# A graph layer's recurrent gates on one Trainium2 core: one scheme of 26 products of 256 columns for gates r and z of a pair of batches

## The chip, the core and the metric

The kernel runs on one core of a Trainium2 chip. The core has a matrix engine (PE, with its weight loads listed apart as PEld), a vector engine (DVE), a scalar engine (ACT), a general engine (POOL) and an engine that issues transfers (SP); each works through its own queue in order, and semaphores tie the queues together. Matrix products land in PSUM, eight banks of 128 x 512 floats; everything else lives in SBUF. The metric is the device time of one execution, in microseconds (us). A smaller time is better.

## The reference

The input x holds 32 batches of 512 tokens by 256 channels, all in float32. After a layer norm and a ReLU (h), each batch goes through three branches that meet in a GRU cell:

```
xc     = transpose(h)
x_conv = relu(bn2(conv17(relu(bn1(conv1(xc))))) + xc)          # convolution branch
A      = exp(-dist(h @ w_se.T)) * adj
x_nmp  = A @ relu(h @ w_msg.T + b_msg)                         # message branch
gi     = concat(x_conv, x_nmp) @ w_ih.T + b_ih                 # 768 columns: r, z, n
gh     = h @ w_hh.T + b_hh
r      = sigmoid(gi_r + gh_r);  z = sigmoid(gi_z + gh_z)
n      = tanh(gi_n + r * gh_n)
out    = x + (1 - z) * n + z * h
```

## The kernel before

Work is staged. Up to 836 us the kernel prepares what the gates need, for two groups of 16 batches: norm, first convolution and a transform to frequencies (`first_part`), the products with the frequency weights and the message branch (`nodes`). In `first_part` of the second group it also combines the gate weights (`combine_weights`, L591): POOL sums and ACT copies on 384-column tiles, spread over 15 batches, and one store of 1344 KB to DRAM for each of the three inputs. What the last stage needs lies in DRAM: h (`HD`), x_nmp (`ND`), the convolution's spectrum (`YD`) and the combined weights (`WS`).

The last stage, from 836 us to the end, is a loop over 16 pairs of batches, and it is where the change is. For a pair p:

- `load_pair` brings h (tile `HP`, "hp" in the profile), x_nmp (`NP`, "np") and the spectrum (`YT`, "yt"). All are channel-major: four row blocks of 512 tokens, block 2*i+j for channel half i and batch j of the pair.
- `inverse` (L661) turns the spectrum back into x_conv: per batch and channel half five products into one bank, then one DVE operation (L673) and one ReLU on ACT (L675) into `CP` ("cp").
- `sums` (L655) makes four sums of blocks on POOL for each of the three operands (L659): with them a 2 x 2 by 2 x 2 block product takes seven products, not eight (Strassen's scheme in Winograd's form).
- `gates_rz` (L687) does gates r and z. For each gate o the seven products run over the three operands k (h, x_nmp, x_conv), each one matmul of 128 x 128 weights on 512 columns. Two gates with two batches each are the four schemes of seven: 2 x 7 x 3 = 42 matmuls. DVE adds (L700, L712, L720), ACT copies (L707) and sigmoids (L696) finish them.
- `gate_n` (L797) does gate n in the same way, 21 matmuls; h's part has a bank of its own since r multiplies it. For each of the four blocks (i, j) DVE does up to four operations (`scaled`, `closing`) and ACT a tanh (L820). Then come three DVE operations for each block, d = h - n (L851), d *= z (L871) and n += d (L872, `blend`).
- `finish` transposes the result back to tokens on DVE (L878), adds x (L883) and stores it.

The order of work is written out by hand (`manual_schedule`): each engine runs its instructions as the program emits them. In the loop (L1197) PE's order is gates r and z of p, then `inverse(p + 1)`, then gate n of p: x_conv of the next pair is done one gate ahead of its first use. Inputs `HP`, `NP` and `CP` have two buffers each, so POOL's twelve sums for p + 1 (eight at `between(1)`, four behind `inverse`) never write where gates of p still read. `RZ` (r and z) has one buffer. A bank is taken by `bank(name)` from a pool of eight.

The last pair (p = 15) does r, then n, then z, with a tail of its own (`last_z`).

Of the kernel before, what the change touches and what calls it, by code (L numbers as in the profile page):

```python
# [15 lines left out]
P = 128  # L16
# [11 lines left out]
ROWS = 2 * UNITS  # L28

# [36 lines left out]
def gnn_layer(  # L66
# [168 lines left out]
    WS = [dram.tile([P, 7, 3, P], FP, name=f"ws_{k}") for k in range(K3)]  # L235
# [355 lines left out]
    def combine_weights():  # L591

        steps = []
        for k, src in enumerate((w_hhT, w_ihT[D:], w_ihT[:D])):
            w, t = (pools["sums"].tile([P, n, 3 * P], FP, tag=f"w{n}", name=f"w{n}_{k}", bufs=m) for n, m in ((4, 1), (7, 2)))
# [14 lines left out]
            for (dst, x1, x2, op), kept in zip(  # L610
                ((Q5, a21, a22, ALU.add), (Q6, q[Q5], a11, ALU.subtract),
                 (Q7, a11, a21, ALU.subtract), (Q3, a12, q[Q6], ALU.subtract)),
                ((Q1, a11), (Q2, a12), (Q4, a22), None),
            ):
                steps.append([partial(nc.gpsimd.tensor_tensor, q[dst], x1, x2, op=op)])
                if kept:
                    steps[-1].append(partial(nc.scalar.copy, q[kept[0]], kept[1]))
            steps[-1].append(partial(nc.sync.dma_start, WS[k], t.rearrange("p q (g o) -> p q g o", o=P)))
        return steps

    def load_combined(sw, q0, q1):
        for k in range(K3):
            nc.gpsimd.dma_start(sw[:, k, q0:q1], WS[k][:, q0:q1])

    def load_pair(p, queue=nc.sync):
        YT[p] = [pools["ops"].tile([P, len(spans), D], FP, tag="yt", name=f"yt_{p}_{j}", bufs=4) for j in range(2)]
        HP[p] = pools["ops"].tile([P, 8, N], FP, tag="hp", name=f"hp_{p}")
        NP[p] = pools["ops"].tile([P, 7, N], FP, tag="np", name=f"np_{p}")
        for j in range(2):
            b = 2 * p + j  # L630
            queue.dma_start(HP[p][:, j:4:2], HD[b])
# [3 lines left out]
        for j in range(2):  # L635
            queue.dma_start(NP[p][:, j:4:2], ND[2 * p + j])

    def load_pair_x(p):

        XP[p] = []  # L640
        for b in (2 * p, 2 * p + 1):
            t = pools["work"].tile([P, N // 32, D // 4], FP, tag="x", name=f"xb_{b}", bufs=3)
# [7 lines left out]
    def operands(t, keep):  # L650

        t3 = 7 if keep else B12
        return [t[:, i, :] for i in (B11, 5, B21, t3, 4, 6, B22)]

    def sums(t, keep):  # L655
        t3 = 7 if keep else B12
        sub = ALU.subtract
        for dst, a, b in ((4, B12, B11), (5, B22, 4), (6, B21, 5), (t3, B22, B12)):
            nc.gpsimd.tensor_tensor(t[:, dst, :], t[:, a, :], t[:, b, :], op=sub)  # L659

    def inverse(p):  # L661

        CP[p] = pools["ops"].tile([P, 7, N], FP, tag="cp", name=f"cp_{p}")
        for j in range(2):
            for oc in range(DC):
# [7 lines left out]
                nc.vector.scalar_tensor_tensor(xc, bk, scale2[:, oc : oc + 1], HP[p][:, 2 * oc + j, :],  # L673
                                               op0=ALU.mult, op1=ALU.add)
                nc.scalar.activation(xc, xc, AF.Relu, bias=shift2[:, oc : oc + 1], scale=1.0)  # L675
        del YT[p]

    def into(bk, q, o, ks, terms, first, t=slice(0, N)):

        for i, k in enumerate(ks):  # L680
            nc.tensor.matmul(bk[:, t], sw[:, k, q, o, :], terms[k][q][:, t], start=(first and i == 0), stop=(i == len(ks) - 1),  # L681
                             skip_group_check=True)

    def temp(role, name):
        return pools["late"].tile([P, N], FP, tag=role, name=f"{role}_{name}", bufs=2)

    def gates_rz(p, terms, between, outs=range(2)):  # L687
        if 0 in outs:
            RZ[p] = pools["late"].tile([P, 2 * DC, 2, N], FP, tag="rz", name=f"rz_{p}", bufs=1)
# [43 lines left out]
    def last_z(p, terms):  # L733
# [13 lines left out]
        def turned(i, j, t=slice(0, N)):  # L747
            dst, (js, half) = d[:, i, j, t], places(i, t)
            nc.vector.tensor_mul(dst, dst, d[:, DC + i, j, t])
            if (p, j) not in OUT:  # L750
                OUT[p, j] = pools["late"].tile([P, N // 32, D // 4], FP, tag="o", name=f"o_{p}_{j}", bufs=2)
# [45 lines left out]
    def gate_n(p, terms, last):  # L797
        rz, o = RZ[p], 2
        NT[p] = nt = pools["late"].tile([P, DC, 2, N], FP, tag="nt", name=f"nt_{p}", bufs=2)
# [7 lines left out]
        def scaled(bk, other, other_i, i, j):  # L807

            n = nt[:, i, j, :]
            if other is None:  # L810
                nc.vector.scalar_tensor_tensor(n, bk, b_hn[:, i : i + 1], rz[:, i, j, :], op0=add, op1=mul)
            else:
                nc.vector.scalar_tensor_tensor(n, bk, b_hn[:, i : i + 1], other, op0=add, op1=add)
                nc.vector.tensor_mul(n, n, rz[:, i, j, :])
                nc.vector.tensor_add(n, n, other_i)

        def closing(bk, i, j):
            n = nt[:, i, j, :]
            nc.vector.tensor_add(n, n, bk)  # L819
            nc.scalar.activation(n, n, AF.Tanh, bias=b_in[:, i : i + 1], scale=1.0)  # L820
# [12 lines left out]
        scaled(x1[0], None, None, 0, 0)  # L833
        closing(x1[1], 0, 0)
        pair(Q7, x2, False)
        u3 = [temp("u3", f"n{p}_{k}") for k in range(2)]
        for k in range(2):
            nc.vector.tensor_add(u3[k], p1[k], x2[k])
        x3 = [bank(f"pn3_{p}_{k}") for k in range(2)]
        pair(Q5, x3, True)  # L840
        scaled(x3[0], u3[0], u3[1], 1, 1)
        closing(x3[1], 1, 1)
        pair(Q4, x2, False)
        scaled(x2[0], p1[0], p1[1], 1, 0)
        closing(x2[1], 1, 0)
        pair(Q3, x3, False)
        scaled(x3[0], u2[0], u2[1], 0, 1)
        closing(x3[1], 0, 1)
        for i, j in ((0, 0), (1, 1), (1, 0), (0, 1)):

            (nc.gpsimd if last else nc.vector).tensor_tensor(rz[:, i, j, :], HP[p][:, 2 * i + j, :], nt[:, i, j, :],  # L851
                                                             op=ALU.subtract)
            if last and j == 0:
                early_out(p, i, j)
            elif not last:

# [403 lines left out]
```

## Time and profile before

| | |
|---|---|
| median of 2 runs | 1801.93 us (1801.38 to 1802.48) |
| the profiled execution, whole | 1803.28 us |
| its span, first to last instruction | 1801.4 us, granted PE clock 0.999 |
| last stage, first matmul of `inverse(0)` to the end | 835.9 to 1801.4 us |
| gates r and z of one pair, first matmul to the next stage's first | 36.05 us (1140.12 to 1176.17) |
| `inverse` of one pair | 5.65 us (1116.45 to 1122.10) |
| gate n of one pair | 18.02 us (1122.10 to 1140.12) |
| store of combined weights, one operand | 1344 KB, 7.3 us to landing |
| load of h, x_nmp, spectrum (SP's queue) | 512 KB 6.1 us, 512 KB 8.8 us, 640 KB 6.7 us to landing, each twice a pair |

The table's times are of one execution. In the timeline a group of matmuls has the start of its first record and a length whose end is modelled and overlaps the next; the distance from one start to the next is what PE needs. A float32 matmul leaves two records. A line of the timeline is: start in us, length in us, engine, source line, operation, output and input tiles, shape, how many were merged, and in brackets the engine's idle time before it with what ended it.

### The profile page before, as it was taken

How to read it: one execution, taken by the hardware profiler on the slowest of the kernel's cores; microseconds unless marked ns; L12 is line 12 of the kernel's file. 1: busy time of each engine (PE TensorE's matmuls, PEld its weight loads, DVE VectorE, ACT ScalarE, POOL GpSimd, SP SyncE). 2: the span in 40 equal slices, each digit the busy share in tenths (PEclk: the TensorE clock that was granted, in tenths of full speed). 3: DMA queues.
4: the chain of work that ended last, by engine and by line, in shares of the span. 5: the costliest groups of instructions: out<-in, count | busy, mean ns of one | idle time of the engine just before them, and what ended most of it. 6: DMA issues, size and time to landing. Idle time of an engine off the chain costs nothing.

```text
span 1801.4 us, 21211 instructions
## 1 busy us (share of the span) xinstructions
PE 1786.5 (99%) x6974; PEld 1148.8 (64%) x6974; DVE 1209.5 (67%) x2242; ACT 635.8 (35%) x1348; POOL 789.7 (44%) x733
## 2 busy tenths in 40 slices
PE   8999999999999999999999999999999999999998
PEld 6677888888998888885554555455545554555443
DVE  7885877886996777873456645665566556655666
ACT  4556554553345544543221222122212221222121
POOL 3432877877334878786123133213321332133221
PEclk9999999999999999999999999999999999999999
DMA  9999989786769889879043234323442344224402
GB/s 257 307 296 232 243 237 231 227 220 203 243 224 224 245 217 234 245 201 319 5 123 106 47 93 123 111 49 86 123 116 55 74 123 116 65 65 123 122 21 51
DMA packets 307089, 288.27 MB, mean 160 GB/s; under 512 B 146764, under 2 KB 237420, under 8 KB 306596
## 3 DMA queue, kind: packets, MB, share of 16 engines
q1 hardware_dynamic: 296948, 261.44, 53.8%
q0 software_dynamic: 6592, 23.50, 4.2%
q10 hardware_dynamic: 3440, 1.97, 0.4%
q8 instruction: 56, 0.92, 0.2%
q14 instruction: 53, 0.43, 0.1%
HBM read 190.45 MB, written 96.40 MB: 159 GB/s over the span
## 4 chain that ended last, share of the span: by engine, by line
PE 94%; DVE 2%; issue 1%; DMA 1%; POOL 1%; ACT 1%; ACTq 0%; SPq 0%; DVEq 0%; POOLq 0%
PE pg L681 30%; PE pn L681 15%; PE py L400 12%; PE pn L555 10%; PE pm L451 6%; PE pc L336 6%; PE pc L669 5%; PE px L351 3%; PE pd L493 2%; PE pw L260 2%; PE phT L316 1%; PE pz L681 1%; PE pn L538 1%; PE psr L475 1%; DMA w2p<-in_w2T_dram 0%
## 5 line engine op out<-in xcount | busy, mean ns | idle before, releaser
L659 POOL TENSOR_TENSOR hp<-hp 128x512 f32<-128x512 f32 x64 | 80.5, 1269 | 414.6 <-DMA hp<-hd 324.4
L681 PE MATMUL pg<-hp,sw 128*128 128x512 f32 x434 | 221.8, 593 | 0.7 <-DVE rz L700 0.5
L681 PE MATMUL pg<-np,sw 128*128 128x512 f32 x434 | 221.6, 592 | 0.0
L681 PE MATMUL pg<-cp,sw 128*128 128x512 f32 x434 | 221.6, 592 | 0.0
L659 POOL TENSOR_TENSOR cp<-cp 128x512 f32<-128x512 f32 x64 | 80.6, 1269 | 227.4 <-ACT cp L675 226.2
L696 ACT ACTIVATE rz<-rz,brz 128x512 f32<-128x512 f32 x93 | 67.0, 721 | 260.2 <-DVE rz L700 260.2
L367 POOL TENSOR_TENSOR wsum<-wt 128x512 f32<-128x512 f32 x78 | 112.0, 1436 | 102.4 <-DMA wt<-wd 61.9
L400 PE MATMUL py<-wt,xf 128*128 128x256 f32 x640 | 154.2, 384 | 0.0
L681 PEld LDWEIGHTS pg<-hp,sw 128*128 128x128 f32 x434 | 82.2, 190 | 104.7 <-issue 97.8
L681 PEld LDWEIGHTS pg<-cp,sw 128*128 128x128 f32 x434 | 82.5, 190 | 103.8 <-issue 103.8
L681 PEld LDWEIGHTS pg<-np,sw 128*128 128x128 f32 x434 | 82.5, 190 | 103.8 <-issue 103.8
L400 PEld LDWEIGHTS py<-wt,xf 128*128 128x128 f32 x640 | 117.1, 190 | 34.9 <-issue 19.7
L503 DVE TENSOR_TENSOR A<-A,at 128x512 f32<-128x512 f32 x124 | 132.9, 1110 | 1.2 <-ACT A L499 1.1
L820 ACT ACTIVATE nt<-nt,vech 128x512 f32<-128x512 f32 x64 | 46.2, 722 | 236.1 <-DVE nt L819 236.1
L336 PE MATMUL pc<-w,hT 128*128 128x256 f32 x512 | 118.0, 383 | 0.9 <-DVE hT L320 0.9
L451 PE MATMUL pm<-wmsg,hq 128*128 128x259 f32 x512 | 117.5, 381 | 0.0
L681 PE MATMUL pn<-cp,sw 128*128 128x512 f32 x224 | 114.4, 592 | 0.0
L681 PE MATMUL pn<-np,sw 128*128 128x512 f32 x224 | 114.4, 592 | 0.0
L681 PE MATMUL pn<-hp,sw 128*128 128x512 f32 x224 | 114.4, 592 | 0.0
L336 PEld LDWEIGHTS pc<-w,hT 128*128 128x128 f32 x512 | 94.6, 190 | 24.2 <-issue 7.2
L451 PEld LDWEIGHTS pm<-wmsg,hq 128*128 128x128 f32 x512 | 96.5, 189 | 14.7
L669 PEld LDWEIGHTS pc<-back,yt 128*128 128x128 f32 x640 | 92.7, 190 | 7.7 <-issue 7.7
(175 smaller groups left out, 3373.5 us busy)
## 6 DMA issues: line engine op xcount, KB each, us to landing
wt<-wd SPq DMA_DIRECT2D x80, 512.0 KB, 7.4
adj<-in_adj_dram SPq DMA_DIRECT2D x128, 256.0 KB, 6.7
wd<-wst SPq DMA_DIRECT2D x64, 320.0 KB, 5.9
yd<-y SPq DMA_DIRECT2D x76, 256.0 KB, 5.1
yt<-yd SPq DMA_DIRECT2D x30, 640.0 KB, 6.7
hd<-hT SPq DMA_DIRECT2D x32, 512.0 KB, 4.5
nd<-nmp SPq DMA_DIRECT2D x32, 512.0 KB, 3.0
xb<-in_x_dram SPq DMA_DIRECT2D x128, 128.0 KB, 3.8
```

The source lines that it names most:

```text
L336: nc.tensor.matmul(p[:, j, :], HT[b][:, ic, c * P : (c + 1) * P], w1[:, ic, :], start=(ic == 0), stop=(ic == DC - 1))
L351: nc.tensor.matmul(p[:, j * 2 * L : (j + 1) * 2 * L], H1[b][:, c0 + j, ic * P : (ic + 1) * P], fwd, start=True, stop=True)
L367: nc.gpsimd.tensor_tensor(t, WT[g, u][:, 0], WT[g, u][:, 1], op=ALU.add)
L400: nc.tensor.matmul(dst, v[:, ic, :], w[:, ic, :], start=(ic == 0), stop=(ic == DC - 1))
L451: nc.tensor.matmul(p[:, : D + NS], hq[:, ic, c * P : (c + 1) * P], wmsg[:, ic, :], start=(ic == 0), stop=(ic == DC - 1))
L503: nc.vector.tensor_mul(A[b][:, mc, :], EXP.pop((b, mc)), AT.pop((b, mc)))
L555: nc.tensor.matmul(bk, left[:, k, :], right[:, k, :], start=(first and k == 0), stop=(k == 1), skip_group_check=True)
L659: nc.gpsimd.tensor_tensor(t[:, dst, :], t[:, a, :], t[:, b, :], op=sub)
L669: nc.tensor.matmul(bk[:, t0:t1], YT[p][j][:, c, oc * P : (oc + 1) * P], back[:, n : n + t1 - t0], start=(c == 0), stop=(c == len(spans) - ...
L681: nc.tensor.matmul(bk[:, t], sw[:, k, q, o, :], terms[k][q][:, t], start=(first and i == 0), stop=(i == len(ks) - 1), skip_group_check=True)
L696: nc.scalar.activation(rz[:, g, j, :], src, AF.Sigmoid, bias=brz[:, g : g + 1], scale=1.0)
L820: nc.scalar.activation(n, n, AF.Tanh, bias=b_in[:, i : i + 1], scale=1.0)
```

## The change

Gates r and z of a pair (p = 0 to 14) are computed as one block product, four output blocks (two gates, two halves) by two input halves by four column blocks of 256 tokens (two batches, two halves), in 26 products (`gates_rz26`). Each is three matmuls of 128 x 128 weights on 256 columns: 78 matmuls of 256 columns take the place of 42 of 512. `PRODUCTS` lists them in order: the operand, an earlier product onto whose bank it accumulates, ACT copies of a bank into a slot (t), DVE additions, and outputs that become a sigmoid one product later.

The operands are blocks of the inputs (b), halves of the four pair sums as before (t3, t4, r5, r6) and ten sums of blocks (E0 to E9). POOL makes all of them: for h and x_nmp together eight operations on 128 x 512 for the pair sums and ten on 128 x 2 x 256 for the E, and for x_conv four on 128 x 512 and ten on 128 x 256. `SUMS_AHEAD` is emitted ahead of gate n, `SUM_ORDER` behind `inverse(p + 1)`.

The tiles of sums (`TN`, `TE`, `TNC`, `TEC`), `CP`, `NT`, `RZ` and the output tile have one buffer each; h and x_nmp share a tile `HN` in two alternating places; `YT` and the x tile have two in place of four and three. `inverse(p + 1)` moves from in front of gate n to behind it, directly ahead of the next pair's gates. In gate n the DVE operations write intermediate values into banks, tanh goes into a bank, and the blends of blocks (0, 0) and (1, 1) are done between the products, those of (1, 0) and (0, 1) among the operations of `inverse(p + 1)`.

`combine_weights` makes 28 more weight blocks for each of the three operands (20 POOL sums and 8 ACT copies of 128 columns), in tiles of one buffer where the seven-product tile had two, and stores 448, 896 and 1664 KB an operand in place of 1344. The last pair keeps the seven-product schemes, its r and z weights loaded into the place of the 26 on SP's queue once gates r and z of pair 14 are done.

```diff
+PRODUCTS = (
+    ('b01', None, 't0=p0', '', ''),
+    ('b03', None, 't1=p1', '', ''),
+    ('b11', None, 't2=p2', 'c11=p2+t0', 'c11=c11'),
+    ('b13', 1, '', '', 'c33=p1'),
+    ('r5_1', None, '', 't3=t0-p4', ''),
+    ('E9', None, '', 't0=t1+p5', ''),
+    ('E8', None, 't1=p6', '', ''),
+    ('t3_1', None, '', 't4=p7-t1 t5=p7-t3', ''),
+    ('E4', None, '', 't1=p8-t0 c23=p8+t4', ''),
+    ('E6', None, '', 't6=p9+t2', ''),
+    ('E7', None, '', 't2=p10-t1', ''),
+    ('r6_0', None, '', 't1=p11-t2 c22=t1-t6', ''),
+    ('E5', None, 't7=p12', '', ''),
+    ('E3', 11, '', 'c21=p11-t6', ''),
+    ('t4_0', None, '', 'c12=p14-t6', ''),
+    ('r5_0', None, '', 't6=p15+t1', ''),
+    ('r6_1', None, '', 'c01=p16-t5', 'c01=c01'),
+    ('t4_1', None, '', 't1=t7+p17 c03=p17-t5', 'c03=c03'),
+    ('t3_0', None, '', 't5=p18-t6 c02=p18-t1', ''),
+    ('E2', None, '', 't6=p19+t4 t7=t6-t5 c12=c12+t7', 'c12=c12'),
+    ('E0', None, '', 'c10=p20-t7 c30=p20+t2', '-c10=c10 c30=c30'),
+    ('b00', None, '', 't2=p21-t6 c22=c22-t2 c23=c23-p21', 'c20=t2 -c23=c23'),
+    ('b13', 17, '', 'c13=p17+t3', 'c13=c13'),
+    ('b12', None, '', 't2=p23-t1 t3=t0-t2 c21=c21-t3', 'c21=c21 c31=t3'),
+    ('b10', 20, '', 'c00=p20+t5', '-c00=c00'),
+    ('E1', None, '', 't0=p25+t2 c02=c02+p25 c22=c22+t0', '-c02=c02 -c22=c22 c32=t0'),
+)
+BLOCK_SUMS = {
+    'E9': ('b11', '+', 'b12'),
+    'E0': ('b10', '-', 'E9'),
+    'E4': ('b00', '-', 'b03'),
+    'E8': ('E4', '+', 'b13'),
+    'E2': ('E8', '-', 'b10'),
+    'E7': ('E4', '-', 'E0'),
+    'E6': ('t4_0', '+', 'E0'),
+    'E5': ('b12', '-', 't4_1'),
+    'E1': ('b02', '-', 't4_1'),
+    'E3': ('E1', '-', 'E7'),
+}
+PAIR_SUMS = {"t4": (1, 0), "r5": (3, "t4"), "t3": (3, 1), "r6": (2, "r5")}
+SUMS_AHEAD = ("E9", "E0", "E4", "E8", "E2", "E7")
+SUM_ORDER = (
+    ('t3', 'hn'), ('t4', 'hn'), ('E6', 'hn'), ('E5', 'hn'), ('E1', 'hn'), ('E3', 'hn'), ('r5',
+    'hn'), ('r6', 'hn'), ('t4', 'c'), ('r5', 'c'), ('E9', 'c'), ('E4', 'c'), ('E8', 'c'), ('t3',
+    'c'), ('E0', 'c'), ('E6', 'c'), ('E7', 'c'), ('r6', 'c'), ('E5', 'c'), ('E1', 'c'), ('E3', 'c'),
+    ('E2', 'c'),
+)
...
-            w, t = (pools["sums"].tile([P, n, 3 * P], FP, tag=f"w{n}", name=f"w{n}_{k}", bufs=m) for n, m in ((4, 1), (7, 2)))
+            w, t, u = (pools["sums"].tile([P, n, m], FP, tag=f"w{n}", name=f"w{n}_{k}", bufs=1)
+                       for n, m in ((4, G // 2), (7, G // 2), (len(PRODUCTS) + 2, P)))
...
+            more = [partial(nc.gpsimd.tensor_tensor, block(dst), block(x), block(y), op=op)
+                    for dst, x, y, op in (v for text in WEIGHT_SUMS for v in terms_of(text))]
+            same = [partial(nc.scalar.mul, block(dst), block(x.lstrip("-")), -1.0 if x[0] == "-" else 1.0)
+                    for dst, x, y, op in (v for text in WEIGHT_COPIES for v in terms_of(text))]
...
+                steps[-1] += spread(more, n, 4) + spread(same, n, 4)
+            parts = t.rearrange("p q (g o) -> p q g o", o=P)
+            for dst, part in ((WN[:, :, k], parts[:, :, 2]), (WL[:, :, k], parts[:, :, :2]), (WH[:, :, k], u[:, : len(PRODUCTS)])):
+                steps[-1].append(partial(nc.sync.dma_start, dst, part))
...
+    def place_sums(p):
+        TN[p] = pools["tn"].tile([P, 4, 2, N], FP, tag="tn", name=f"tn_{p}", bufs=1)
+        TE[p] = pools["te"].tile([P, len(EXTRA), 2, HALF], FP, tag="te", name=f"te_{p}", bufs=1)
+        TNC[p] = pools["tnc"].tile([P, 4, N], FP, tag="tnc", name=f"tnc_{p}", bufs=1)
+        TEC[p] = pools["tec"].tile([P, len(EXTRA), HALF], FP, tag="tec", name=f"tec_{p}", bufs=1)
+
...
+    def sums_ahead(p):
+        for name in SUMS_AHEAD:
+            block_sum(p, name, "hn")
+
+    def sums(p, last):
+        for name, part in SUM_ORDER[p == 0 :]:
+            if not (last and name in BLOCK_SUMS):
+                block_sum(p, name, part)
+
...
+    def inverse(p, between=()):
+
+        between = list(between)
+        CP[p] = pools["cp"].tile([P, 4, N], FP, tag="cp", name=f"cp_{p}", bufs=1)
...
+                for step in between.pop(0) if between else ():
+                    step()
+        for step in (v for w in between for v in w):
+            step()
...
+    def gates_rz26(p, between):
+
+        rz = RZ[p] = pools["rz"].tile([P, 2 * DC, 2, N], FP, tag="rz", name=f"rz_{p}", bufs=1)
+        slots = CT.rearrange("p r (h n) -> p (r h) n", h=2)
+        banks, waiting = {}, []
+
...
+        for s, (name, onto, copies, adds, done) in enumerate(PRODUCTS):
+            if onto is None:
+                banks[s] = bank(f"pg_{p}_{s}")
+            bk = banks[s if onto is None else onto][:, :HALF]
+            hn, c = operand(p, name, "hn"), operand(p, name, "c")
+            for k in range(K3):
+                nc.tensor.matmul(bk, SW["hk"][:, s, k, :], c if k == 2 else hn[:, k], start=(onto is None and k == 0),
+                                 stop=(k == K3 - 1), skip_group_check=True)
+            for dst, src, *_ in terms_of(copies):
+                nc.scalar.copy(at(dst), at(src))
+            sigmoids()
+            for dst, x, y, op in terms_of(adds):
+                nc.vector.tensor_tensor(at(dst), at(x), at(y), op=op)
+            for word in done.split():
+                dst, src = word.lstrip("-").split("=")
+                waiting.append((dst, src, -1.0 if word[0] == "-" else 1.0))
+            for step in between.get(s, ()):
+                step()
+        sigmoids()
+
...
+        def finished(banks, other, spare, i, j):
+
+            n, r = nt[:, i, j, :], rz[:, i, j, :]
+            (bk, bk_i), (h, g) = banks, spare
             if other is None:
-                nc.vector.scalar_tensor_tensor(n, bk, b_hn[:, i : i + 1], rz[:, i, j, :], op0=add, op1=mul)
+                nc.vector.scalar_tensor_tensor(n, bk, b_hn[:, i : i + 1], r, op0=add, op1=mul)
+                nc.vector.tensor_add(n, n, bk_i)
             else:
-                nc.vector.scalar_tensor_tensor(n, bk, b_hn[:, i : i + 1], other, op0=add, op1=add)
-                nc.vector.tensor_mul(n, n, rz[:, i, j, :])
-                nc.vector.tensor_add(n, n, other_i)
+                nc.vector.scalar_tensor_tensor(h, bk, b_hn[:, i : i + 1], other[0], op0=add, op1=add)
+                nc.vector.tensor_mul(n, h, r)
+                nc.vector.tensor_add(g, other[1], bk_i)
+                nc.vector.tensor_add(n, n, g)
+            NEW[p, i, j] = n if last else g
+            nc.scalar.activation(NEW[p, i, j], n, AF.Tanh, bias=b_in[:, i : i + 1], scale=1.0)
 
...
-        scaled(x1[0], None, None, 0, 0)
-        closing(x1[1], 0, 0)
+        finished(x1, None, x1, 0, 0)
         pair(Q7, x2, False)
         u3 = [temp("u3", f"n{p}_{k}") for k in range(2)]
         for k in range(2):
             nc.vector.tensor_add(u3[k], p1[k], x2[k])
+        if not last:
+            for step in blend(p, 0, 0):
+                step()
         x3 = [bank(f"pn3_{p}_{k}") for k in range(2)]
         pair(Q5, x3, True)
-        scaled(x3[0], u3[0], u3[1], 1, 1)
-        closing(x3[1], 1, 1)
+        finished(x3, u3, x1, 1, 1)
         pair(Q4, x2, False)
-        scaled(x2[0], p1[0], p1[1], 1, 0)
-        closing(x2[1], 1, 0)
+        finished(x2, p1, x2, 1, 0)
+        if not last:
+            for step in blend(p, 1, 1):
+                step()
         pair(Q3, x3, False)
-        scaled(x3[0], u2[0], u2[1], 0, 1)
-        closing(x3[1], 0, 1)
...
+    def blend(p, i, j):
+        n, d = NEW.pop((p, i, j)), RZ[p][:, i, j, :]
+        return [partial(nc.vector.tensor_tensor, d, HN[p][:, 0, 2 * i + j, :], n, op=ALU.subtract),
+                partial(nc.vector.tensor_tensor, d, d, RZ[p][:, DC + i, j, :], op=ALU.mult),
+                partial(nc.vector.tensor_tensor, NT[p][:, i, j, :], d, n, op=ALU.add)]
 
...
+    homes = ("rz", "nt", "ct", "sw", "yt", "hn0", "te", "tn", "tnc", "tec", "cp", "hn1", "swn", "xb", "o")
+    with phase(*homes), tc.manual_schedule():
         pairs = B // 2
-        sw = pools["sw"].tile([P, K3, 7, 3, P], FP, name="sw")
+        CT = pools["ct"].tile([P, 6, N], FP, tag="ct", name="ct", bufs=1)
+        TURN, NEW = {}, {}
         load_pair(0, nc.gpsimd)
-        load_combined(sw, 0, 2)
-        sums(HP[0], True)
-        load_combined(sw, 2, 7)
-        sums(NP[0], False)
+        load_combined(0, 5)
+        place_sums(0)
+        sums_ahead(0)
+        load_combined(5, 12)
+        block_sum(0, *SUM_ORDER[0])
+        load_combined(12, 26)
+        load_n()
         inverse(0)
-        sums(CP[0], False)
+        sums(0, False)
         for p in range(pairs):
             more = p + 1 < pairs
-            if more:
-                load_pair(p + 1)
-            terms = [operands(HP[p], True), operands(NP[p], False), operands(CP[p], False)]
 
             def between(i):
                 if p > 0:
                     finish(p - 1, i)
                 if i == 1:
                     load_pair_x(p)
-                    if more:
-                        sums(HP[p + 1], True)
-                        sums(NP[p + 1], False)
-
+
+            terms = [operands(p, k) for k in range(K3)]
             if more:
-                gates_rz(p, terms, between)
-                inverse(p + 1)
-                sums(CP[p + 1], False)
+                steps = {4: [partial(load_pair, p + 1)]}
+                if p > 0:
+                    steps[3] = [partial(to_tokens, p - 1, 0, 0)]
+                    steps[5] = [partial(to_tokens, p - 1, 0, 1)]
+                    steps[6] = [partial(finish, p - 1, 0)]
+                    steps[7] = [partial(to_tokens, p - 1, 1, 0)]
+                    steps[8] = [partial(to_tokens, p - 1, 1, 1)]
+                    steps[9] = [partial(finish, p - 1, 1)]
+                steps[12] = [partial(load_pair_x, p)]
+                gates_rz26(p, steps)
+                place_sums(p + 1)
+                last = p + 2 == pairs
+                if last:
+                    load_last()
+                else:
+                    sums_ahead(p + 1)
                 gate_n(p, terms, False)
+                (s0, s1, s2), rest = blend(p, 1, 0), blend(p, 0, 1)
+                inverse(p + 1, [[s0], [s1], [s2], rest])
+                sums(p + 1, last)
```

## The prediction

> **What bounds the kernel now.** I read the page first: busy times and the chain that ended last.
>
> ```profile
> PE 1786.5 (99%) x6974; PEld 1148.8 (64%) x6974; DVE 1209.5 (67%) x2242; ACT 635.8 (35%) x1348; POOL 789.7 (44%) x733
> ...
> PE 94%; DVE 2%; issue 1%; DMA 1%; POOL 1%; ACT 1%; ACTq 0%; SPq 0%; DVEq 0%; POOLq 0%
> ```
>
> PE never stops, so the time is PE's own work, and a change has two terms: what PE has less to do, and where PE now has to wait. For the first, the timeline of PE, in the frequency products (256 columns) and in the gates (512):
>
> ```profile
> 421.80 1.89 PE L400 MATMUL py<-wt,xf 128*128 128x256 f32 x8
> 423.53 1.03 PE L400 MATMUL py<-wsum,both 128*128 128x256 f32 x4
> ...
> 1103.57 1.02 PE L681 MATMUL pg<-hp,sw 128*128 128x512 f32 x2
> 1104.43 1.02 PE L681 MATMUL pg<-np,sw 128*128 128x512 f32 x2
> ```
>
> From start to start, eight records (four matmuls) of 256 columns take 1.73 us, 0.4325 each; one of 512 takes 0.858. Half the columns cost half the time, with the same weight loads, so the shorter matmul has no penalty here.
>
> For the second term, the timeline of all engines where gate n of pair 14 ends. I call T the moment PE ends gate n, here 1737.34:
>
> ```profile
> 1730.67 0.75 DVE L813 SCALAR_TENSOR_TENSOR nt<-pn,vech,u_n 128x512 f32<-128x512 f32 x1 [0.17 <-PE pn L681]
> ...
> 1736.49 0.74 DVE L813 SCALAR_TENSOR_TENSOR nt<-pn,vech,u_n 128x512 f32<-128x512 f32 x1
> ...
> 1737.34 1.02 PE L681 MATMUL pg<-hp,sw 128*128 128x512 f32 x2
> ...
> 1738.79 0.69 DVE L819 TENSOR_TENSOR nt<-nt,pn 128x512 f32<-128x512 f32 x1
> 1739.39 0.68 DVE L851 TENSOR_TENSOR rz<-hp,nt 128x512 f32<-128x512 f32 x1
> ...
> 1741.45 0.69 DVE L851 TENSOR_TENSOR rz<-hp,nt 128x512 f32<-128x512 f32 x1
> ```
>
> From 1730.67 on DVE has no idle time: it ends gate n at T + 2.1 (1739.48), and then the blends, 2.06 us each (1739.39 to 1741.45), run beside the next pair's gates. Nobody waits for them. Later in the same timeline stand a wait for a one-buffer tile and a collision:
>
> ```profile
> 1748.57 2.13 POOL L872 TENSOR_TENSOR nt<-nt,rz 128x512 f32<-128x512 f32 x1
> 1750.74 0.69 ACT L696 ACTIVATE rz<-pg,brz 128x512 f32<-128x512 f32 x1 [9.98 <-POOL nt L872]
> ...
> 1769.51 0.69 DVE L815 TENSOR_TENSOR nt<-nt,u_n 128x512 f32<-128x512 f32 x1
> 1771.83 1.68 POOL L851 TENSOR_TENSOR rz<-hp,nt 128x512 f32<-128x512 f32 x1 [4.42 <-ACT nt L820]
> 1772.41 1.64 DVE L815 TENSOR_TENSOR nt<-nt,p_n 128x512 f32<-128x512 f32 x1
> ```
>
> The sigmoid writes block (0, 0) of the new `RZ`; POOL was reading other blocks of the old one. So a one-buffer tile comes free as a whole, after its last reader. And L815, two inputs in SBUF, takes 1.64 us beside a POOL sum, not 0.69, the sum 1.68, not 1.27.
>
> **PE's work.** 42 x 0.858 = 36.05 us become 78 x 0.4325 = 33.74: 2.31 us less a pair, 34.7 us over the fifteen pairs. That is 1.9% of 1801.9, and all that the change can give.
>
> **Where PE waits: x_conv comes late.** `inverse(p + 1)` now stands straight before the gates that read it, behind gate n on PE and DVE, and two blends move into gate n. DVE then ends gate n at T + 2.1 + 2 x 2.06 - 0.17 (its one gap) = T + 6.1. `inverse` takes PE 5.65 us; its first bank is full at T + 1.4, but the L673 that empties it queues behind gate n on DVE. L673 takes 0.75 and the ReLU 0.72, so the first x_conv block is there at T + 7.6. The first product wants it in its third matmul, at T + 5.65 + 2 x 0.4325 = T + 6.5: a wait of 1.2 with the hand-over. The second product wants the block that is emptied third; on DVE lie L673, blend step, L673, blend step, L673 (0.75, 0.72, 0.75, 0.73, 0.75), so T + 9.8, and 10.6 after the ReLU, where PE, late by 1.2, asks at T + 9.0: 1.6 more. So 2.8 us a pair is the least.
>
> Banks: a pair takes 22 in its products, 6 in gate n, 4 in `inverse`, 32 in all. If the eight go round, the second product gets the bank in which the tanh of block (1, 0) lies, read last by that blend's third step, behind the third L673: T + 10.4. The product then starts at 10.5 instead of T + 8.15: 2.35 in place of 1.6. No row shows the order of banks; I take the round, 3.5 us in sum.
>
> Collision: two d *= z (both inputs in SBUF) stand in this DVE queue ahead of the second product, while POOL sums without a pause. Each costs 0 to 0.95 (the row above); the mask product L503 in the message stage, beside a busy POOL, means 1110 ns, 0.42 more than a lone operation. I take 0.5 each: 1.0.
>
> POOL's sums: `TN` has one buffer, so its first sum waits for gate n's last read, the second matmul of its sixth product, T - 3.4. Then come fourteen operations to r5 of x_conv, which the fifth product wants. At 1.28 us (hp's four sums, 5.2 us) it is done at T + 14.6, at np's 1.5 (6.06 for four) at T + 17.6. PE, late by 4.5, asks at T + 11.7 + 4.5 = 16.2: 0 to 1.4, I take 0.3. Later sums are 0.74 to 1.28 each and PE asks for one every 1.3 us. In sum 3.5 + 1.0 + 0.3 = 4.8 us a pair, 72 us over the fifteen hand-overs; at least 2.8 (42), at most 3.5 + 1.9 + 1.4 = 6.8 (102).
>
> **First pair.** POOL does twenty sums before r5 of x_conv, 25.6 us and three load issues of 0.54, from about 822 to 826 (hp's sums began at 824.6): done at 849 to 853, wanted at 841.5 + 6.1 = 847.6. I take 3 us (1 to 6).
>
> **Combined weights.** Each of twelve batches gets five more POOL sums of 128 columns; 384 columns take 0.99 us, 256 take 0.73, so 0.4 to 0.73 each, 2 to 3.7 us, which fits POOL's idle 3.5 before each rstd. But the four normalising DVE operations (L308) take 2.12 us beside one such sum (at 480.03) and 1.46 beside none (486.37), and DVE is busy 18.2 to 19.7 of each 20 us there. 0 to 1.2 a batch, 0.5 taken: 6 us. The stores are 3008 KB, not 1344; at 7.3 us for 1344 they land after 16.3, while the next operand's first sum and copy, now in the same buffer, came 12.2 us behind the store (481.0 to 493.2). So POOL and ACT may wait 4 us, twice, with L340's ReLUs and L354's copies queued behind on ACT: 2 us (0 to 8). Together 8 (0 to 22).
>
> **At nothing.** DVE in the gates: 35 additions of 0.41, four transposes of 0.69, two additions of 1.45, 20 of 33.7 us. ACT: 16 sigmoids of 0.51 and 5 copies of 0.39 for 8 and 2 longer ones, busy 35%. SP: the six loads of `load_pair` are issued behind product 5, land within some 15 us and are wanted 27 us later; the x load waits for the stores of its two buffers, and behind it SP has nothing due for a gate. Without that cover it would be some 9 us, np's landing, a pair. The last pair's weights, 2688 KB, have the 23.7 us of gate n and `inverse`.
>
> **Sum.** -34.7 + 72 + 3 + 8 = +48. On the profiled execution (1803.28, span 1801.4 and 1.9 around it) 1851; it lies 1.35 over the median, so 1850. With all low ends 1810, with all high ends 1897.
>
> Beside this sum, two rules. The Trainium skill (SBUF — State Buffer, Who interferes with whom) says that a DVE instruction with two SBUF inputs and a reading POOL instruction lock each other out for a whole instruction. By it each d *= z could wait a whole sum, 1.27 us, not 0.5, and the time would be 1873. The granted clock is 1.00 in every stretch to 1760 us and 0.94 in the last 42, where PE works 33. The skill (TensorE: Matmul & The Clock Gate, What's actually happening) halves PE's clock after an idle window of some 3.4 us. Two waits of 1.2 and 3.3 us leave it whole; should one outgrow the window, 3.4 us at half rate would by estimate cost 1.7 a pair, 26 in all.
>
> **Rivals.** (1) x_conv is in time, and the change is faster. The mechanism is DVE's queue at T; it decides at 2.31 us of waiting a pair. For it: DVE has gaps early in gate n (2.75 and 1.01 us at L831), and the new forms work from banks, clear of POOL. Against it: none of those gaps lies behind 1730.67, where the delay builds. With 0 to 1 us of waits: 1770 to 1786. (2) POOL decides: its 22 sums of 1.28 and ten of 0.74 are 36 us a pair, where it was 15, and over three quarters fall after T - 3.4. If collisions hold it at np's rate, r5 of x_conv sets the hand-over, 6.1 to 7 us a pair, from T + 16.2 on: 1870 to 1885. (3) The weight stage blocks ACT for longer than a store: some 1880. That the 26 products don't spare PE what they say is excluded by the rows of 256 columns.
>
> **Chances.** Forecast 0.70, rival 1 0.15, rival 2 0.11, rival 3 0.04. Two per cent, about what a measurement of this kernel can tell from no change, is 1766 to 1838. Of the forecast some 0.26 lies under 1838; with rival 1's 0.12, 0.38 for no change. Rival 1 passes 1766 only with nothing lost and a shorter tail: 0.03. Slower: 0.44 + 0.11 + 0.04 = 0.59. The range 1804 to 1890 leaves out rival 1 and 0.05 above.
>
> **What would show it.** Gates of a pair span about 33.7 us and the waits; PE's idle time sits in the first two products, ended by ACT's ReLU of `CP` and a DVE blend step, less by POOL at the fifth; L673 starts some 5 us after its bank is full. PE idle by POOL through many products speaks for rival 2, gapless gates for rival 1.

## The result and the profile after

The changed kernel takes 1851.12 us, median of 2 runs (1849.72 to 1852.52), beside 1801.93: ratio 1.027, 95% interval 1.023 to 1.032, slower. The profiled execution took 1849.72, its span 1847.9 us. Split at the first matmul of `inverse(0)`:

| us | before | after | difference | on record |
|---|---|---|---|---|
| stages up to `inverse(0)` | 835.9 | 853.1 | +17.2 | +8 |
| last stage | 965.5 | 994.8 | +29.3 | -34.7 + 72 + 3 = +40 |

So the total came out right by two errors that cancel, +9.2 in the first row and -10.7 in the second. First the page of after, busy times and chain:

```profile
PE 1775.3 (96%) x8054; PEld 1355.9 (73%) x8054; DVE 1334.1 (72%) x2621; ACT 671.7 (36%) x1537; POOL 1131.0 (61%) x1087
...
PE 74%; POOL 15%; DVE 5%; issue 3%; DMA 2%; SPq 1%; ACT 1%; ACTq 0%; POOLq 0%; DVEq 0%
```

PE is idle for 73 us of the span, where it was for 15, and POOL, which had 1% of the chain, has 15%. The list of PE's waits (total, times, longest) names where it stops:

```profile
PE pg L856 <- ACT cp L823: 32.1, 28, 1.7
PE pg L856 <- POOL tnc L763: 15.9, 15, 2.1
PE phT L385 <- DVE xn L377: 4.7, 3, 2.6
```

L856 are the gates' matmuls, L823 the ReLU of `inverse`, L763 POOL's sums, L385 the transposes in the weight stage. Two waits a pair for x_conv, one for a sum. One hand-over in the timeline of PE, T = 1221.86:

```profile
1221.86 5.81 PE L817 MATMUL pc<-back,yt 128*128 128x136 f32 x40
1227.51 1.03 PE L856 MATMUL pg<-hn,sw 128*128 128x256 f32 x4
1229.10 0.70 PE L856 MATMUL pg<-cp,sw 128*128 128x256 f32 x2 [0.57 <-ACT cp L823]
1229.64 1.03 PE L856 MATMUL pg<-hn,sw 128*128 128x256 f32 x4
1232.39 0.70 PE L856 MATMUL pg<-cp,sw 128*128 128x256 f32 x2 [1.73 <-ACT cp L823]
...
1235.58 1.03 PE L856 MATMUL pg<-tn,sw 128*128 128x256 f32 x4
1237.58 0.70 PE L856 MATMUL pg<-tnc,sw 128*128 128x256 f32 x2 [0.98 <-POOL tnc L763]
```

Two matmuls need 0.865 us from start to start. The first, second and fifth product stop 0.73, 1.89 and 1.14 longer between their h and x_conv lines, and each stop costs another 0.1 before the next line: 4.1 us. From one `inverse` to the next are 61.47 us, where before had 59.72. The same stretch on DVE:

```profile
1226.94 0.69 DVE L1011 TENSOR_TENSOR nt<-nt,pn 128x512 f32<-128x512 f32 x1
1227.55 0.74 DVE L821 SCALAR_TENSOR_TENSOR cp<-pc,bn_scale,hn 128x512 f32<-128x512 f32 x1
...
1229.47 1.45 DVE L825 TENSOR_TENSOR rz<-rz 128x512 f32<-128x512 f32 x1
1230.84 0.74 DVE L821 SCALAR_TENSOR_TENSOR cp<-pc,bn_scale,hn 128x512 f32<-128x512 f32 x1
1231.50 0.67 DVE L825 TENSOR_TENSOR nt<-rz,pn 128x512 f32<-128x512 f32 x1
```

Gate n's last operation (L1011) stands directly ahead of the first emptying of a bank (L821), which starts at T + 5.7. The third L821, for the second product's block, comes behind a d *= z (L825) of 1.45 us, 0.76 more than a lone one: POOL was summing beside it. POOL itself:

```profile
1218.67 4.97 POOL L761 TENSOR_TENSOR tn<-hn 128x512 f32<-128x512 f32 x4 [7.19 <-PE pn L873]
...
1236.26 1.26 POOL L763 TENSOR_TENSOR tnc<-cp,tnc 128x512 f32<-128x512 f32 x1
```

It stood idle for 7.19 us until gate n's sixth product (T - 3.2), and ended r5 of x_conv at 1237.52, T + 15.7.

### The profile page after: what moved, and what is told of

Read it like the earlier page. It is cut to its first block, busy times and chain, and to the rows that moved or that the text cites. A ratio compares the mean times of both kernels' runs of the same rounds, so it can differ in the third digit from the quotient of the medians.

```text
span 1847.9 us, 24424 instructions
## 1 busy us (share of the span) xinstructions
PE 1775.3 (96%) x8054; PEld 1355.9 (73%) x8054; DVE 1334.1 (72%) x2621; ACT 671.7 (36%) x1537; POOL 1131.0 (61%) x1087
## 3 DMA queue, kind: packets, MB, share of 16 engines
q8 instruction: 64, 1.05, 0.2%
## 4 chain that ended last, share of the span: by engine, by line
PE 74%; POOL 15%; DVE 5%; issue 3%; DMA 2%; SPq 1%; ACT 1%; ACTq 0%; POOLq 0%; DVEq 0%
PE pg L856 23%; PE pn L873 13%; PE py L469 11%; PE pn L624 10%; POOL tn L761 7%; PE pm L520 5%; POOL te L763 4%; PE pc L405 3%; POOL tnc L763 3%; PE px L420 2%; PE pd L562 2%; PE pw L329 2%; DMA w<-in_w_ihT_dram 1%; DVE xn L377 1%; PE pg L873 1%
## 5 line engine op out<-in xcount | busy, mean ns | idle before, releaser
L763 POOL TENSOR_TENSOR te<-hn 128x512 f32<-128x512 f32 x30 | 38.0, 1267 | 230.8 <-PE pg L856 224.7
L761 POOL TENSOR_TENSOR tn<-hn 128x512 f32<-128x512 f32 x64 | 79.5, 1275 | 131.4 <-PE pn L873 131.4
L847 ACT ACTIVATE rz<-rz,brz 128x256 f32<-128x256 f32 x180 | 86.5, 504 | 196.9 <-DVE rz L862 196.9
L856 PE MATMUL pg<-te,sw 128*128 128x256 f32 x600 | 155.3, 382 | 0.0
L856 PEld LDWEIGHTS pg<-te,sw 128*128 128x128 f32 x600 | 114.9, 191 | 15.9
L856 PE MATMUL pg<-hn,sw 128*128 128x256 f32 x480 | 124.0, 381 | 0.0
L856 PE MATMUL pg<-tn,sw 128*128 128x256 f32 x480 | 123.2, 379 | 0.0
L873 PE MATMUL pn<-tn,sw_n 128*128 128x512 f32 x256 | 120.3, 592 | 0.0
L856 PE MATMUL pg<-cp,sw 128*128 128x256 f32 x240 | 74.3, 391 | 32.1 <-ACT cp L823 32.1
L856 PEld LDWEIGHTS pg<-tn,sw 128*128 128x128 f32 x480 | 91.2, 190 | 12.4
L856 PEld LDWEIGHTS pg<-hn,sw 128*128 128x128 f32 x480 | 88.9, 190 | 13.7 <-ACT ct L859 2.7
```

The source lines that it names most:

```text
L761: nc.gpsimd.tensor_tensor(dst[:, k], x[:, k], y[:, k], op=op)
L763: nc.gpsimd.tensor_tensor(dst, x, y, op=op)
L847: nc.scalar.activation(at(dst), at(src), AF.Sigmoid, bias=brz[:, o : o + 1], scale=sign)
L856: nc.tensor.matmul(bk, SW["hk"][:, s, k, :], c if k == 2 else hn[:, k], start=(onto is None and k == 0), stop=(k == K3 - 1), skip_group_ch ...
L873: nc.tensor.matmul(bk[:, t], weight(q, k, o), terms[k][q][:, t], start=(first and i == 0), stop=(i == len(ks) - 1), skip_group_check=True)
```

## The experiments

All run beside the kernel before on the same chip (its medians 1802.5 to 1803.8).

**The order of x_conv's blocks.**

```diff
-        for j in range(2):
-            for oc in range(DC):
+        for oc in range(DC):
+            for j in range(2):
```

> Only the order in which inverse makes its four blocks changes: channel half outside, batch inside, so that block 1, which the second product wants, is emptied second and not third. Theory (two waits of nearly the same end, DVE's queue and POOL's sums): the wait for the ReLU in the second product (1.73 us a pair) goes, but r5 of x_conv still ends at T + 15.6 because POOL's queue does not move, and PE now waits there for some 3 us instead of 1: 0.2 us a pair, about 3 in all, 1848 us (1844 to 1851). Rival (DVE's queue alone sets the hand-over, POOL's 1 us is a by-product): the 1.9 us a pair go for good, 28 us, 1823 us.

Measured 1850.43 us (1848.61 to 1852.58): the total is as the theory said, and DVE's queue alone doesn't set the hand-over. A pair takes what it took in the changed kernel, 61.47:

```profile
1160.67 5.81 PE L817 MATMUL pc<-back,yt 128*128 128x136 f32 x40
...
1222.14 5.81 PE L817 MATMUL pc<-back,yt 128*128 128x136 f32 x40
```

But the wait that took over isn't the one I named. POOL's waits stayed at 15.8 us, and 15.2 us in 14 waits came new from ACT's copies (L859). The fourth product fills on the bank of the second, and must wait until ACT has copied that out; the copy stands behind four ReLUs. That is a third late queue.

**TN in four tiles.**

```diff
-        TN[p] = pools["tn"].tile([P, 4, 2, N], FP, tag="tn", name=f"tn_{p}", bufs=1)
+        TN[p] = [pools["tn"].tile([P, 2, N], FP, tag=f"tn{r}", name=f"tn{r}_{p}", bufs=1) for r in range(4)]
```

> Only the tile TN changes: four tiles of one row each in place of one of four, with the same bytes, so that POOL may write t3 and t4 of the next pair once gate n's fourth and fifth products have read the old ones. Theory: POOL starts its pair sums some 4 to 7 us sooner, r5 of x_conv then follows the third ReLU (T + 10.5) and is done at about T + 13.5, before PE, late by 2.7 through x_conv, asks for it at T + 14.4: the 1.1 us a pair at the fifth product go, x_conv's waits stay, 17 us, 1834 us (1828 to 1840). Rival (POOL is what holds the hand-over, as in the third row of rivals): all 4.1 us a pair go, 1790 us. If TN's release as a whole does not matter: 1851 us.

Measured 1828.16 us (1827.19 to 1829.05), 23 us less. PE's waits for POOL fell from 15.9 us to 2.0, the first pair's alone, as expected; beyond that x_conv's fell from 32.1 to 27.5, since POOL's h and x_nmp sums now end before that d *= z begins, which took 0.68 us. A pair takes 59.90 us.

**Both.**

> Both edits of the two runs before in one kernel. Theory (two queues late by about the same): more than the sum of the two alone, since each uncovers the other. Left are the wait for the first ReLU, 0.7 us a pair, and some 0.5 at r5 of x_conv (done at T + 13.0, asked at T + 12.5), so 2.8 us a pair go, 42 us, 1809 us (1800 to 1818). If the two waits were independent of each other, the gains of the two runs alone would add up and no more.

Measured 1827.16 us (1824.77 to 1829.13), 24 us less than the changed kernel and no more than the two gains together (0.7 and 23). The theory missed by 18 us, and most of that, 14.2, is the third queue. PE's waits:

```profile
PE pg L856 <- ACT cp L823: 14.3, 14, 1.0
PE pg L856 <- ACT ct L859: 14.2, 14, 1.0
```

One first ReLU and one copy a pair, 1.0 us each. Both go back to when DVE gets to `inverse`.

**DVE's queue at T.** On top of that, the closing operations of block (0, 1) go behind the first L821, the blend of (1, 1) behind `inverse`:

```diff
-                gate_n(p, terms, False)
-                (s0, s1, s2), rest = blend(p, 1, 0), blend(p, 0, 1)
-                inverse(p + 1, [[s0], [s1], [s2], rest])
+                closing = gate_n(p, terms, False)
+                inverse(p + 1, [[closing]])
+                for step in (v for i, j in ((1, 1), (1, 0), (0, 1)) for v in blend(p, i, j)):
+                    step()
```

> On top of the kernel with both edits (1827 us, last stage 971 us, waits of 1.03 us for the first ReLU and 1.02 us for ACT's copy of the second product, which stands behind four ReLUs and whose bank the fourth product fills on): on DVE the first operation of inverse now stands ahead of gate n's closing operations of block (0, 1), and the blend of (1, 1) stands behind inverse with the other two. Theory (DVE's queue at T is the root of both waits, ACT's copies are late only since the ReLUs are): the first x_conv block is there at T + 3, the copies at about T + 8.7, POOL's r5 of x_conv at T + 10.3, all before PE asks (T + 6.5, T + 9.6, T + 11.7); the 2.2 us a pair go, 30 us, 1797 us (1793 to 1803). Rival (a next queue is late by as much: the nine blend operations push DVE's additions to T + 14, and PE stops for a bank or for POOL): half of it, 1810 us or more.

Measured 1816.98 us (1815.33 to 1817.20), the rival's side. Both waits are gone and one came in their place, at the fourteenth product, which fills on the twelfth's bank once a DVE addition has read it (PE's timeline, T = 1212.20):

```profile
1234.25 0.59 PE L856 MATMUL pg<-tec,sw 128*128 128x256 f32 x2
1236.65 1.13 PE L856 MATMUL pg<-te,sw 128*128 128x256 f32 x4 [1.81 <-DVE ct L862]
```

DVE did nine blend operations and then additions mixed with the finishing of the pair before, without a gap from T + 1.7 to T + 24.8. Either it has too much to do in all, or only in this stretch:

```diff
-                    steps[3] = [partial(to_tokens, p - 1, 0, 0)]
+                    steps[13] = [partial(to_tokens, p - 1, 0, 0)]
...
-                    steps[9] = [partial(finish, p - 1, 1)]
-                steps[12] = [partial(load_pair_x, p)]
+                    steps[18] = [partial(finish, p - 1, 1)]
+                steps[21] = [partial(load_pair_x, p)]
```

> On top of the kernel with the late closing (1817 us; one wait a pair left, 1.8 us for a DVE addition): only the end of the pair before, four transposes and two additions on DVE with the stores behind them, moves from behind products 3 to 9 to behind products 13 to 18, and the load of x from product 12 to 21. Same work. Theory (DVE is late only in the stretch of the first ten products, into which the nine blend operations were pushed; over a pair it has room): with 5.7 us of finishing out of that stretch its additions catch up before the eighth bank is asked for; the wait goes, 1.9 us a pair, 27 us, 1790 us (1786 to 1797). Rival (DVE is the bound over the whole of the gates, and the wait comes back at a later product or in gate n): 1808 us or more.

Measured 1790.88 us (1790.41 to 1792.71), ratio 0.9935 (0.992 to 0.995): only in this stretch. The steady pairs have no wait left.

**The weight stage.** In the changed kernel POOL, PE's transposes and the granted clock, in two views (timeline; stretches with PE's busy time, clock, DMA share and GB/s):

```profile
500.21 2.24 POOL L1197 TENSOR_TENSOR w<-w 128x384 f32<-128x384 f32 x4 [5.51 <-DMA w<-in_w_ihT_dram]
...
506.43 2.62 PE L385 MATMUL phT<-ident,xn 128*128 128x128 f32 x8 [2.55 <-DVE xn L377]
```

```profile
506.00:508.00 2.00, 1.57 (x5) 0.50 0.50 203
508.00:510.00 2.00, 2.00 (x8) 0.50 0.12 16
```

POOL waits for the next operand's weights, the normalisation's factor (`rstd`) behind it on POOL is late, PE stops for 2.55 us, and then its clock is 0.50. First the sums were made in another order, so that blocks 0 to 18 and the seven-product weights go out one batch sooner; of the edit, the line of the stores:

```diff
+                steps[-1] += stores[:3] if n == 2 else stores[3:] if n == 3 else []
```

> Only the weight stage changes: the sums are made in another order, so that blocks 0 to 18 of the 26 and the seven-product weights are complete and stored one batch sooner; behind the last sums of an operand only 448 KB go to DRAM ahead of the next operand's load, not 3008. Same sums, same bytes. Theory: of the 17 us that the stages before the last one are longer, POOL's waits for the next operand's weights (5.5 and 6.6 us), the late normalisation behind them and PE's slow clock after the stop are the larger part: 9 us less (5 to 13), 1842 us. Rival (the 60 more sums beside the DVE are what costs): 0 to 3 us less, 1848 to 1851.

Measured 1850.11 us (1849.12 to 1851.51). The load was issued 3.4 us later (489.67 for 486.24), behind a store of the transposed h that waits for DVE, and landed at the same time, 500.1. The theory wasn't tested. The load was then given to ACT's queue:

```diff
+            queue = nc.scalar if k > 0 else nc.sync
```

> On top of the kernel with the early stores (1850 us): the loads of the second and third operand's weights are issued by ACT right behind its last copies, not by SP, where they stood behind a store that waits for the transposed h. In the run before, the load was issued at 489.7 and landed at 500.1, while POOL asked at 496.1. Theory (POOL's block on this load is the larger part of the 17 us): issued at about 485.8, landed at 495 to 496, POOL's waits of 4.1 and 6.0 us fall under 1, PE's stops of 2.5 us in front of the transposes of the two batches behind them go with the slow clock after them: 8 us less (4 to 12), 1842 us. Rival (the sums themselves, beside the DVE, cost the time): within 2 us of 1850.

Measured 1848.12 us (1844.76 to 1848.51), the rival's figure. POOL's wait for the weights fell to 0.5 us and none, and the time hardly moved: now DVE waited for other transfers (its waits from 438 to 552 us):

```profile
DVE stats L358 <- DMA x<-in_x_dram: 8.0, 3, 4.0
DVE hT L389 <- DMA hd<-hT: 6.5, 2, 3.4
```

In the changed kernel these two are 3.5 and 5.6 us. So another transfer came late in place of the first. The suspect is the burst of 3008 KB, beside which the DMA share was 1.07 (490 to 500 us, changed kernel). Last, the same bytes in five pieces, with the sums reordered to suit and the loads still on ACT's queue (two parts of the edit):

```diff
+                *((WH[:, s0:s1, k], u[:, s0:s1]) for s0, s1 in ((0, 12), (12, 20), (20, 26)))))
...
+                (((Q5, a21, a22, ALU.add), (Q6, q[Q5], a11, ALU.subtract)), ((Q1, a11), (Q2, a12)), same[:2], []),
+                (((Q7, a11, a21, ALU.subtract), (Q3, a12, q[Q6], ALU.subtract)), ((Q4, a22),), same[2:5], [wl]),
+                ((), (), same[5:7], [wn, wh[0]]),
+                ((), (), same[7:], [wh[1]]),
```

> The changed kernel with another weight stage alone: blocks are made in another order and stored in five pieces of 384 to 896 KB over four batches, in place of 3008 KB behind the last batch of an operand, and the next operand's weights are loaded from ACT's queue. Same sums, same bytes. Theory (the burst holds up whatever transfer stands beside it: the weights in the changed kernel, the store of the transposed h and the load of x in the run from ACT's queue): DVE's waits for these two transfers fall from 14 us to 4 or less, PE's stops of over 2 us go but the first, 9 us less (6 to 13), 1842 us. Rival (the sums themselves are what costs, or the total of bytes): 1847 to 1851.

Measured 1840.38 us (1837.50 to 1841.62), ratio 1.0203 (1.0186 to 1.0220), 10.7 us less than the changed kernel and 7.7 less than the run from ACT's queue; `inverse(0)` starts at 845.9 and not 853.1. The store of h no longer holds DVE at all, the load of x still does for 5.6 us. The sums' collisions with DVE aren't the cost: in the changed kernel the normalising operations (L377) average 552 ns, 541 before (L308), 0.6 us over 56 of them. Whether POOL's own time for the sums is part of the 10.0 us that are left (845.9 for 835.9) is not shown.

**Sums of edits.** Late closing and ACT's queue:

> The edits of the two runs before together. They lie in different stages, so their gains add: 1797 and 8 less, 1789 us (1784 to 1798), which would be 0.7% faster than the kernel before. If either theory falls, 1797 to 1812.

Measured 1814.49 us (1812.56 to 1819.33): both had fallen short. Late closing, late finishing and spread stores:

> The edits of both runs before together (hand-over and finishing; weight stage): 1790 and 9 less, 1781 us (1775 to 1797), faster than the kernel before by some 1.2%. If only the hand-over theory holds, 1788 to 1790; if only that of the weight stage, 1805.

Measured 1778.00 us (1776.75 to 1779.17), ratio 0.9862 (0.9847 to 0.9876), the fastest kernel here: clear of the kernel before, though by less than two per cent. Its page, and one pair from `inverse` to `inverse` on PE:

```profile
PE 1755.7 (99%) x8054; PEld 1357.6 (76%) x8054; DVE 1325.5 (75%) x2621; ACT 668.7 (38%) x1537; POOL 1111.2 (63%) x1087
```

```profile
1191.42 5.81 PE L821 MATMUL pc<-back,yt 128*128 128x136 f32 x40
...
1248.76 5.81 PE L821 MATMUL pc<-back,yt 128*128 128x136 f32 x40
```

57.34 us with no stop, 2.38 less than before; PE is back at 99%.

**POOL alone.** In this kernel TN is put back into one tile.

> The fastest kernel so far (1778 us, no wait left in a steady pair) with one thing put back: TN is one tile of four rows again, so POOL's pair sums start only behind gate n's sixth product, at T - 3.3. Everything else stays in time. Theory (the two late queues ran side by side in the changed kernel, each hiding most of the other): r5 of x_conv ends at T + 15.6 as it did there, PE asks at T + 11.7, so POOL alone costs 3.8 us in each of 14 hand-overs, 53 us, 1831 us (1820 to 1838), though in the changed kernel PE was seen waiting for it only 1.0 us a pair and taking that wait away gave 23 us. Rival (the waits stand one behind the other and add up): 23 us, 1801 us.

Measured 1857.85 us (1851.78 to 1862.17), 80 us more, slower than the changed kernel itself:

```profile
1228.98 1.03 PE L860 MATMUL pg<-tn,sw 128*128 128x256 f32 x4
1233.87 1.22 PE L860 MATMUL pg<-tnc,sw 128*128 128x256 f32 x2 [3.86 <-POOL tnc L767]
1234.89 1.91 PE L860 MATMUL pg<-te,sw 128*128 128x256 f32 x4
```

POOL ends r5 of x_conv at T + 15.7 as in the changed kernel, and PE waits 3.86 us, 54 us over 14 hand-overs (56 with the first pair's): the theory's size, against the rival's 23; but the total lies outside its 1820 to 1838. On top comes what I had not counted: after that stop two matmuls (four records) take 1.91 us in place of 1.03, at a granted clock of 0.61 from 1235 to 1240, and what needs 3.03 us at full rate takes 5.57 (1233.87 to 1239.44). Over all hand-overs 26 us are left for this and for the restart behind each stop, 1.9 a pair. It differs from pair to pair: after the same stop the clock stayed whole in three hand-overs of fourteen, as here (timeline, and a stretch with PE's busy time, clock, DMA share and GB/s):

```profile
1046.25 0.70 PE L860 MATMUL pg<-tnc,sw 128*128 128x256 f32 x2 [3.86 <-POOL tnc L767]
```

```profile
1046.00:1051.00 5.00, 4.75 (x22) 1.00 1.01 356
```

These pairs take 61.46 to 61.47 us, the other eleven 62.90 to 64.38. And 61.47 is the changed kernel's own pitch: where the clock stays whole, POOL alone costs all that its hand-over cost. In both kernels, and with x_conv's blocks reordered, r5 of x_conv ends at T + 15.7. So in the changed kernel POOL's sum set the length of the hand-over, and x_conv's two waits, twice as long in PE's list, lay in front of it and cost nothing further.

## Why the prediction was right, and where its terms were not

1850 was forecast, 1851 came. The kind of cause is the one forecast: PE has less to do, and loses more than that where `inverse` stands directly ahead of the gates, by late x_conv blocks and a late sum. That the total hit to 1 us is luck, since the last stage came out 10.7 us under its terms and the stages ahead 9.2 over theirs. And of the two waits the one priced at 0.3 set the length of the hand-over. Term by term, with the pitch of a pair without stops (57.34) as the rule:

- **PE's work, -34.7.** Right: 57.34 for 59.72 is -2.38 a pair, -35.7 in fifteen, seen once the waits were gone.
- **The hand-over, 4.8 a pair.** 61.47 less 57.34 is 4.13, 57.8 us over 14, not 15: the hand-over into the last pair is another, with one stop of 2.7 us for POOL. The order of the parts on DVE was right (gate n ended at T + 5.7, I had 6.1; the third ReLU at T + 10.5, I had 10.6), the split was not. The step that failed is "the second product gets the bank in which the tanh of block (1, 0) lies": its h matmuls started at once, at 1229.64, while that blend's third step ran at 1231.50. No bank wait, 0.75 too much. A bank does bind, but another: the second product's, by ACT's copy, seen only when x_conv came sooner. In the time it is r5 of x_conv that counts, as it ends last: the forecast has PE go on at T + 16.2 + 0.3 = 16.5, 4.8 behind the T + 11.7 at which it asks without other waits; r5 came at T + 15.7, which with the restart is the 4.1.
- **Collision, 1.0.** The two d *= z ahead of the second product took 1.05 and 1.45 us, 0.36 and 0.76 more than alone: about right, and within the bounds (0 to 0.95 each); with late closing one took 1.82, 1.13 more. The rule of the Trainium skill (SBUF — State Buffer, Who interferes with whom), a lock for a whole instruction, would let each wait a whole sum, 1.27; these rows show a part of one.
- **POOL's sums, 0.3.** r5 of x_conv at T + 15.7, inside the forecast T + 14.6 to 17.6; PE came sooner, for want of the bank wait, so it stopped 1.1. Whole release of `TN` was the cause, as written and as shown by the four tiles. The prediction had PE come late to this sum through x_conv, and then took for POOL only what was left over, 0.3. By itself POOL is worth 3.9 a pair and, with the restart and the slow clock, 5.8 on average; x_conv by itself, with `TN` in four tiles, is worth 2.6 (59.90 less 57.34). Rival 2, that POOL decides, was nearer than its chance of 0.11 says, though at a smaller size than its 6.1 to 7.
- **First pair, 3.** One stop of 2.10 for POOL and a slow clock after it: 867.03 to 871.84 for what takes 3.03 at full rate; 4.0 in sum.
- **Combined weights, 8 (0 to 22).** 17.2. "0 to 1.2 a batch, 0.5 taken" for collisions is the step that failed: 0.6 us in all. The stores' term, 2 us, was mis-sized: I had them block only POOL and ACT by their own buffers, and they held up h, x and the next weights as well. Spreading them, with the loads on ACT's queue, gave 7 to 13 us back, by the runs that share a weight stage (842.2 to 845.9 in three, 853.1 to 854.8 in six). Left at nothing was PE's clock: of the 17.2 us PE's idle time is 7.9 (13.8 for 5.9), and some 6 more go to a clock of 0.50 from 505.9 to 512.7 and from 577.6 to 584.4 us (an estimate, half of the 12.3 us that PE was busy there). POOL's sums didn't quite fit its idle time either: DVE waits 6.6 us for `rstd`, 1.7 before. How the idle time is shared between stores and sums stays open; in the run with spread stores a stop of 3.68 us behind the first operand's weights is still there.

The parts add to -35.7 + 57.8 + 2.7 + 4.0 = +28.8, measured +29.3. The clock rule that stood beside the sum (the Trainium skill, TensorE: Matmul & The Clock Gate, What's actually happening) was not in play at the hand-over: three stops, the longest 1.73, at a clock of 1.00. When one stop grew to 3.86, the clock cost 0 to 2.9 a pair, 1.6 on average (the mean pitch, 63.10, less 61.47); the estimate had been 1.7 for every pair.

## What to carry to other kernels

Waits that end at nearly the same place hide each other: PE's list showed 32.1 us for x_conv and 15.9 for POOL, yet taking 18 us of the first away gave 0.7, and the second alone, all else in time, cost 80 (some 23 of it by the clock). Taking one queue's delay away showed the next. Size each queue by when it would be ready against when PE asks with no other wait, and expect the gain only when the last of them is in time. When a one-buffer step is moved next to its consumer, move DVE's deferrable work (blends, finishing) out of the stretch where the consumer's inputs queue, and release tiles by the row, not as a whole.

## What the runs showed of the hardware

- The length of a stop doesn't settle whether the clock drops. With late closing, stops of 1.8 us in the steady pairs left it at 1.00, while in the weight stage of the same run stops of 1.70 and 1.64 us were followed by 0.50 (470.2 to 473.4 and 545.3 to 548.5 us). With POOL alone, 3.86 us left it at 1.00 in three hand-overs of fourteen and brought it to 0.50 in the others. The Trainium skill (TensorE: Matmul & The Clock Gate, What's actually happening) gives an idle window of some 3.4 us, free-running. That the same stop has different outcomes fits a free-running window; that stops of half its length are enough doesn't fit the length, and there the measurement decides.
- After each short stop the group behind it starts 0.1 us later than its pitch, 0.3 us for the three of a hand-over.
- Beside stores of 3008 KB in one burst the DMA share was 1.07 (490 to 500 us), and the next operand's weights, the store of h or the load of x came late, which of them differing from run to run. With the same bytes in pieces of 384 to 896 KB, and the loads on ACT's queue, the stages up to `inverse(0)` took 842.2 to 845.9 us in three runs, where the burst had 853.1 to 854.8 in six; ACT's queue with the stores in two parts had 851.6 and 855.9 in two.
